# A two-layer attention and FFN kernel: the opening attention by halves of the heads, context sums cleared at the start, and another order of the gated sums at the end

## The chip, the cores and the metric

The kernel runs on one core of a Trainium2 chip. The metric is the device time of one execution in microseconds (us). Engines are named as in the profile: PE multiplies matrices, DVE and ACT work on vectors, POOL (GpSimd) and SP issue DMAs beside other work.

## The reference

All arrays are f32. `x` and `ctx` are (16, 256, 256): 16 batches of 256 rows of width 256. The mask has one entry per batch, query and key. Two layers each add an attention and a feed-forward part to x, on a layer norm of x without weights.

```python
# layer 0: 16 heads of width 16, keys = values = ctx
q, k, v = heads(layernorm(x)), heads(ctx), heads(ctx)
scores = where(mask == 0, -1e20, einsum('bqhd,bkhd->bhqk', q, k))
attn = softmax(scores / sqrt(256), axis=3)
x = x + einsum('bhqk,bkhd->bqhd', attn, v).reshape(b, l, e) @ W_out.T + b_out
# layer 0 FFN, 256 -> 1024 -> 256; quantization scales need the maximum over all activations
x = x + quant_linear(relu(quant_linear(layernorm(x), w1, b1)), w2, b2)
# layer 1: correlation of q and k by FFT, its mean over batches picks 6 delays, softmax over them,
# then the values shifted by these delays, weighted and projected
x = x + autocorrelation(layernorm(x), ctx, Wq, Wk, Wv, Wo, ...)
# layer 1 FFN: a shared expert, and 8 routed ones of which each token takes 2
t = layernorm(x)
shared = gelu(t @ Wfc_s + bfc_s) @ Wproj_s + bproj_s
routed = sum over e of gate[:, e] * (gelu(t @ Wfc[e] + bfc[e]) @ Wproj[e] + bproj[e])
x = x + shared + routed
```

## The kernel before, in words

x stays in SBUF for the whole program, as 32 tiles of 128 rows. PE's order inside the first attention is written out by hand, piece by piece; the other engines' orders come from a scheduler, which is held by "issue after" edges in places (`behind()` places an instruction after the last reduction issued). SP's queue issues its DMAs in order: an issue that has to wait holds up all behind it.

**Layer 0 attention.** Each batch has 16 heads in four groups of four. `prep(b)` spreads ctx on 32-partition strips (`cxp`, POOL, L431), normalizes x to `qp` (L440), turns the int mask into an added bf16 mask `mb` (DVE, L451), and turns `cxp` and `qp` on PE into `kT` and `qT`. `turn` (L369) does half of such a turn: four transposes into a PSUM tile of a pool with one buffer, and an ACT copy out (L374). `mtp` (L479) turns the mask.

`largest(b, r)` is a *round*: 16 score matmuls (`sp`, L498) into two tiles of the PSUM pool `ps_w` (three buffers) and eight DVE instructions that add the mask and take the row maximum (L509, into `mx`). Four rounds make a batch: `qt, gp = divmod(r, 2)`, so rounds 0 and 1 take the first 128 queries for both halves of the groups, rounds 2 and 3 the other 128. `shift(b)` negates the maxima into `mxc` (L529), turns them on PE (`mxtp`, L538) and writes them into spare rows of `qT` (L547), so that the second score matmul gives scores less their maximum.

A *slot* is one group of a batch. `weights(b, g)` computes transposed scores (`st`, 16 matmuls, L566), adds the mask by four matmuls (L576) and takes two exponentials on ACT (L586). `values` multiplies by the context (`o`, L599) one slot later. `finish(b)`, in pieces spread over the slots of the next batch, transposes `oT` (`otp`, L617), divides by the sums (L624, L625), transposes again (`ontp`, L635), copies on ACT (L641), projects (`pp`, L649) and adds to x (L653). `stats0` computes layer norm statistics ahead. Rounds run ahead of the slots: five rounds ahead from slot 2 on, four in the beginning. Before slot 0 the program does the rounds 0 to 3 of batch 0, with `prep(1)` and the statistics of batch 1 between, and then `shift(0)`.

**Transition to the first FFN.** `keys1(b)` loads ctx, transposes it (`ctp`, L942), copies it reversed to `cT` on ACT (L945), which also sums it into a column of `csum`; then it computes projected keys (`pk`, L954) and stores them in `gT` (ACT, L962). `csum`, and two constants `zsel` and `avg` that the autocorrelation uses much later, are allocated in a pool that takes over the attention's space, and are cleared there on POOL (L875 to L884). Four `keys1` and four `values1` come ahead of the first quantized block (`qi` L995/996, `qtp` L1000, `ph` L927, `hmax` L1008), whose scale needs the maximum over all x (POOL `partition_all_reduce`, L869).

**Tail.** The last part runs the shared expert in 16 units of 256 rows; units 12 to 15 are left for the end, beside the combination of the routed experts' outputs. `shared_fc(u)` (`pfs`, L1512, then gelu L1520), then one unit later `shared_proj(u)` (`pps`, L1552, a PSUM tile for two halves of 128 rows in a pool with two buffers). For the late units each half is added to x by itself (L1561) and sent out (`leave`, L1542). `combine(u)` loads the unit's routed outputs (`yg`, 512 KB, L1686), adds a bias row (L1693) and adds four gated products (L1698). Late units and combines are interleaved by these lines:

```python
pend, late_ones = None, list(range(U0, NU)) + list(range(U0))   # U0 = 12, NU = 16
share = -(-NU // (NU - U0))
```

After each `shared_fc` of a late unit, and after the previous unit's projection, four combines of this list follow; units 0 to 11 are sent out after theirs.

Of the kernel before, what the change touches and what calls it, by code (L numbers as in the profile page):

```python
# [8 lines left out]
F32 = mybir.dt.float32  # L9
# [19 lines left out]
def tile_kernel(ctx: ExitStack, tc: tile.TileContext, io: dict, out: bass.AP):  # L29
# [112 lines left out]

    rows_of = [32 * (b % 4) + b // 4 for b in range(B)]


# [3 lines left out]
    with tc.tile_pool(name="pa", bufs=2) as pa, tc.tile_pool(  # L149
# [213 lines left out]
        mxcs = [pa.tile([P, QT, 4, HP], F32, tag=f"mxc{i}", bufs=1, name=f"mxc{i}") for i in range(2)]  # L363
        def turn(dst, src, g0, name):

            tp = mtile([P, 2, QT, P], f"{name}_tp")
            for g in range(2):
                for t in range(QT):
                    nc.tensor.transpose(  # L369
                        tp[:, g, t, :],  # L370
                        src[:, t, 4 * (g0 + g) : 4 * (g0 + g) + 4, :].rearrange("p h d -> p (h d)"),
                        ident,
                    )
            nc.scalar.copy(  # L374
                dst[:, g0 : g0 + 2, :].rearrange("p g s -> p (g s)"),
                tp.rearrange("p g t q -> p (g t q)"),
            )
# [39 lines left out]
        def prep(b):  # L417
# [30 lines left out]
            if b == 0:  # L448
                order["last"] = last.ins
            with behind():  # L450
                nc.vector.tensor_scalar(mb, mi, 0.0, MASKED, ALU.is_equal, ALU.mult)  # L451
            if b == 2:
# [5 lines left out]
            if near:  # L458
                turn_close(kT, cx, f"kT{b}")
                yield  # L460
                turn_close(qT, qn, f"qT{b}")
                if b + 2 < B:
                    fetch(b + 2)
                yield
            else:
                turn(kT, cxp, 0, f"kT{b}")
                yield
                turn(kT, cxp, 2, f"kT{b}")
                yield
            if b == 0:  # L470
                turn(qT, qp, 0, f"qT{b}")
                yield
                turn(qT, qp, 2, f"qT{b}")
                yield
# [8 lines left out]
            yield  # L483
            if 0 < b < 3:
                turn(qT, qp, 0, f"qT{b}")
                yield
                turn(qT, qp, 2, f"qT{b}")
                yield

        def largest(b, r):  # L490

            pr = seqs[b]
            qt, gp = divmod(r, 2)
            sps = [ps_w.tile([P, 2, 2, S], F32, tag="w", name=f"sp{b}_{r}_{j}") for j in range(2)]
# [26 lines left out]

        def shift(b):

            pr = seqs[b]
            mxc = mxcs[b % 2]
            if b < 2:
                nc.gpsimd.memset(mxc, 0.0)
            with tc.high_priority():
                nc.vector.tensor_scalar(  # L529
                    mxc[:, :, :, HD : HD + G],  # L530
                    pr["mx"].rearrange("p t (g j) -> p t j g", g=G),
                    -1.0,
                    None,
                    ALU.mult,
                )
            tp = mtile([P, QT, P], f"mxtp{b}")
            for t in range(QT):
                nc.tensor.transpose(  # L538
                    tp[:, t, :], mxc[:, t].rearrange("p j c -> p (j c)"), ident
                )  # L540
            with ExitStack() as where:
                where.enter_context(tc.high_priority())
                if b > 0:
                    where.enter_context(tc.issue_after(order["half"]))
                for gs in (slice(0, 1), slice(1, G)) if b == 0 else (slice(0, G),):
                    to = pr["qT"][:, gs, :]
                    done = nc.vector.scalar_tensor_tensor(  # L547
                        to,
                        to,
                        keep,  # L550
                        tp.rearrange("p t q -> p (t q)").unsqueeze(1).to_broadcast(to.shape),
                        ALU.mult,
                        ALU.add,
                    ).ins
            if b == 0:
                order["last"] = done
            yield
# [116 lines left out]
        stats0(0, 1)  # L674
        first_prep = prep(0)
        piece(first_prep)
        load_x(1, 2)
        for _ in range(3):
            piece(first_prep)
        largest(0, 0)  # L680
        piece(first_prep)
        with behind():
            stats0(1, 2)
        first_prep = prep(1)
        piece(first_prep)
        largest(0, 1)
        piece(first_prep)
        piece(first_prep)
        fetch(2)
        load_x(2, 5)  # L690
        fetch(3)
        largest(0, 2)
        largest(0, 3)

# [29 lines left out]
        def load_w(name, eng):  # L724
# [16 lines left out]

        iota_l = early.tile([P, S], F32, name="iota_l")
        nc.gpsimd.iota(
            iota_l, pattern=[[1, S]], base=0, channel_multiplier=0, allow_small_or_imprecise_dtypes=True
        )

# [56 lines left out]

        for _ in shift(0):
            pass
        with behind():
            stats0(2, 3)
        load_x(5, 9)
        pend = None
        for b in range(B + 1):  # L810
            nxt = prep(b + 2) if b + 2 < B else rest
            fin = finish(b - 1) if b > 0 else None
            shf = shift(b + 1) if b + 1 < B else None
            past = summary(b - 2) if b > 1 else None

            jobs = [
                ((nxt,), (rest,), (fin,)),
                ((nxt,), (nxt,), (fin,)),
                ((fin,), (rest,), (fin,)),
                ((shf,), (), (fin,)),  # L820
            ]
            if b == 0:
                jobs = [
                    ((), (), (first_prep,)),
                    ((nxt,), (nxt,), (nxt,)),
                    ((nxt,), (nxt,), (rest,)),
                    ((rest,), (shf,), (rest,)),
                ]
            for r in range(4):

                n = 4 * b + r
                front, later = {0: ([], [4]), 1: ([5], [6])}.get(
                    n, ([n + 5] if n + 5 < 4 * B else [], [])
                )
                for m in front:
                    largest(*divmod(m, 4))
                for job in jobs[r][0]:
                    piece(job)
                if pend is not None:
                    values(*pend)  # L840
                for job in jobs[r][1]:
                    piece(job)
                pend = (b, r, []) if b < B else None
                wts = weights(*pend) if b < B else None
                piece(wts)
                for job in jobs[r][2]:
                    piece(job)
                piece(wts)
                if n == 0:
                    piece(first_prep)  # L850
                for m in later:
                    largest(*divmod(m, 4))
                with behind():
# [3 lines left out]
                    if b > 0 and r != 2:  # L857
                        piece(ints)
                if r == 0 and b % 4 == 0 and b + 9 < B:
                    load_x(b + 9, b + 13)  # L860
# [12 lines left out]
    gp = until_moe.enter_context(tc.tile_pool(name="gp", bufs=1, side="right"))  # L873
    csum = gp.tile([P, DC, P], F32, name="csum")
    nc.gpsimd.memset(csum, 0.0)  # L875

    zsel = gp.tile([P, 63], F32, name="zsel")
    nc.gpsimd.memset(zsel, 0.0)
    nc.gpsimd.memset(zsel[:, 31:32], 1.0 / D)

    avg = gp.tile([P, P], F32, name="avg")
    nc.gpsimd.memset(avg, 0.0)
    for j in range(4):
        nc.gpsimd.memset(avg[32 * j : 32 * j + B // 4, :], 1.0 / B)  # L884

# [242 lines left out]
    with tc.tile_pool(name="pc", bufs=2) as pc:  # L1128

        def diagonals(four):  # L1130

            for b, skew in four:
# [8 lines left out]
                )  # L1141

        queue = []
        for _ in range(3):
# [401 lines left out]
    def shared_proj(u, hT):  # L1546
        wp = shared_w[1]
        t0 = 2 * u
        po = ps_p.tile([P, 2, D], F32, tag="p", name=f"pps{u}")
        for i in range(2):  # L1550
            for fc in range(FC):
                nc.tensor.matmul(  # L1552
# [5 lines left out]
                )  # L1558
            if u >= U0:
                xt = x[:, t0 + i, :]  # L1560
                nc.vector.tensor_tensor(xt, po[:, i, :], xt, ALU.add)  # L1561
                leave(t0 + i)
        if u < U0:
            xu = x[:, t0 : t0 + 2, :]
# [80 lines left out]
    for u in range(U0):  # L1645
# [9 lines left out]
        pend = (u, hT)  # L1655
    shared_proj(*pend)
    until_moe.close()
    mw = ctx.enter_context(tc.tile_pool(name="mw", bufs=3, side="right"))
# [20 lines left out]
    def combine(u):  # L1679
# [11 lines left out]
        )  # L1691
        xu = x[:, t0 : t0 + 2, :]
        nc.vector.tensor_tensor(  # L1693
            xu, xu, bps_row.unsqueeze(1).to_broadcast([P, 2, D]), ALU.add
        )
        for t in range(2):
# [10 lines left out]

    pend, late_ones = None, list(range(U0, NU)) + list(range(U0))
    share = -(-NU // (NU - U0))
    for u in range(U0, NU):  # L1710
        hT = shared_fc(u)
        if pend is not None:
            shared_proj(*pend)
        pend = (u, hT)
        for v in late_ones[:share]:
            combine(v)
            if v < U0:
                leave(2 * v)
                leave(2 * v + 1)
        late_ones = late_ones[share:]  # L1720
    shared_proj(*pend)
# [39 lines left out]
```

## Time and profile before

| | |
|---|---|
| three runs | 1445.36, 1446.9, 1444.29 us, median 1445.36 |
| profiled execution | 1446.0 us, of which the span of the profile is 1444.3 us, at a mean granted clock of 0.987 |
| busy, share of the span | PE 1371.0 us (95%), DVE 642.9 (45%), ACT 539.6 (37%), POOL 239.1 (17%) |
| first st (slot 0) starts | 32.52 us |
| first keys (pk) start | 429.48 us |
| last x add starts | 1440.76 us |

A span counts from the first to the last instruction of the profiled execution, all positions are microseconds from its start, and shares of the span are averages over stages that have different limits. In a timeline a row gives the start, the length, the engine, the line, the operation with its tiles and how many were merged (x), and in brackets the idle time before it and what released it. Rows of waits give the total, the number of times and the longest.

### The profile page before, as it was taken

What the parts mean: (1) busy time and instruction counts of PE and PEld (TensorE: products, weight loads), DVE (VectorE), ACT (ScalarE), POOL (GpSimd) and SP (SyncE); (2) the same over time, 40 slices, a digit from 0 to 9 for tenths busy, and PEclk for the clock granted to TensorE, in tenths of its full rate; (3) what the DMA queues carried; (4) which work ended last, traced back from release to release, by engine and by line L of the source; (5) the groups of instructions that cost most, each with busy time, mean ns of one, the idle gap of its engine ahead of it and who ended that gap; (6) DMA issues with size and microseconds to landing.
All of it is one profiled execution on the core that took longest, in us unless ns stands there. A gap on an engine that the chain in (4) does not pass through costs nothing. (4 is left out here: it accounts for less than half of the span.)

```text
span 1444.3 us, 24031 instructions
## 1 busy us (share of the span) xinstructions
PE 1371.0 (95%) x8881; PEld 1041.8 (72%) x8955; DVE 642.9 (45%) x2553; ACT 539.6 (37%) x1019; POOL 239.1 (17%) x312
## 2 busy tenths in 40 slices
PE   6999999999988899999999999999999999999968
PEld 3566655666546544678688888888888888888857
DVE  7688879887736858847831101011011011011052
ACT  1454545454434367523623222332333333332221
POOL 6233033302000000000025540111111111111100
PEclk9899999999989999999999999999999999999989
DMA  9232323221001100233002245776767767764173
GB/s 276 69 93 65 91 82 102 62 75 21 12 8 45 37 8 1 88 118 86 10 27 74 77 138 201 249 235 240 254 226 245 258 229 242 254 227 167 54 239 116
DMA packets 127832, 184.07 MB, mean 127 GB/s; under 512 B 11600, under 2 KB 104952, under 8 KB 127712
## 3 DMA queue, kind: packets, MB, share of 16 engines
q1 hardware_dynamic: 117600, 152.55, 32.6%
q0 software_dynamic: 10112, 29.94, 6.1%
q8 instruction: 72, 1.18, 0.3%
q14 instruction: 48, 0.39, 0.1%
HBM read 141.16 MB, written 34.48 MB: 122 GB/s over the span
## 5 line engine op out<-in xcount | busy, mean ns | idle before, releaser
L1520 ACT ACTIVATE hTr<-pfr,bsel 128x256 f32<-128x256 f32 (+1 forms) x344 | 147.8, 430 | 345.7 <-PE pfr L1512 336.8
L1611 PE MATMUL ppr<-wp,hTr 128*128 128x256 f32 x1088 | 248.5, 379 | 0.0
L1512 PE MATMUL pfr<-xjT,wf 128*128 128x256 f32 (+1 forms) x1376 | 246.6, 338 | 0.7 <-DVE xjT L1601 0.7
L1512 PEld LDWEIGHTS pfr<-xjT,wf 128*128 128x128 f32 x1376 | 215.8, 191 | 30.3 <-issue 9.9
L1619 DVE TENSOR_TENSOR yj<-ppr,bj 128x512 f32<-128x512 f32 (+1 forms) x43 | 24.9, 580 | 440.3 <-PE ppr L1611 440.3
L1611 PEld LDWEIGHTS ppr<-wp,hTr 128*128 128x128 f32 x1088 | 202.2, 190 | 25.0
L509 DVE CUSTOM_DVE_ANT_0 junk<-sp,mb 128x256 bf16<-128x256 f32 x512 | 182.8, 420 | 37.7 <-PE sp L498 37.4
L586 ACT ACTIVATE pT<-st 128x1024 f32<-128x1024 f32 x128 | 124.4, 1021 | 128.0 <-PE st L576 128.0
L1637 POOL DMA_INDIRECT ys_d<-yj,to x68 | 65.4, 962 | 454.2 <-DVE to L1628 238.2
L1552 PE MATMUL pps<-wp-1_7259,hTs 128*128 128x256 f32 x512 | 117.4, 388 | 13.5 <-DVE x L1561 13.5
L1552 PEld LDWEIGHTS pps<-wp-1_7259,hTs 128*128 128x128 f32 x512 | 99.3, 195 | 28.7 <-DVE x L1561 14.7
L1520 ACT ACTIVATE hTs<-pfs,bcol 128x256 f32<-128x256 f32 x128 | 59.9, 474 | 160.1 <-PE pfs L1512 157.0
L1512 PE MATMUL pfs<-xnT,wf-1_7257 128*128 128x256 f32 x512 | 114.7, 380 | 0.1
L1512 PEld LDWEIGHTS pfs<-xnT,wf-1_7257 128*128 128x128 f32 x512 | 96.6, 190 | 14.2 <-issue 1.4
L498 PE MATMUL sp<-kT,qT 16*128 16x256 f32 x1024 | 93.1, 421 | 3.6 <-DVE mx L509 3.3
L566 PE MATMUL st<-qT,kT 32*128 32x256 f32 x1024 | 79.5, 408 | 0.7 <-DVE qT L547 0.7
L498 PEld LDWEIGHTS sp<-kT,qT 16*128 16x128 f32 x1024 | 59.2, 193 | 26.4 <-DVE mx L509 9.5
L1475 POOL DMA_INDIRECT xs_d<-xn,slot_i x64 | 61.8, 966 | 92.7 <-ACT hTs L1520 49.6
L927 PE MATMUL ph<-qT,w1T 128*128 128x512 bf16 x245 | 68.6, 378 | 7.4 <-DVE hmax L1008 2.8
L599 PE MATMUL o<-pT,cxp 128*32 128x256 f32 x1024 | 73.4, 396 | 1.3 <-ACT pT L586 1.3
L1565 DVE TENSOR_TENSOR x<-pps,x 128x512 f32<-128x512 f32 x12 | 8.3, 690 | 128.0 <-PE pps L1552 128.0
L566 PEld LDWEIGHTS st<-qT,kT 32*128 32x128 f32 x1024 | 51.4, 189 | 18.5 <-issue 12.6
(304 smaller groups left out, 1622.0 us busy)
## 6 DMA issues: line engine op xcount, KB each, us to landing
wf<-in_L_ffn_Wfc_dram SPq DMA_DIRECT2D x43, 1024.0 KB
wp<-in_L_ffn_Wproj_dram SPq DMA_DIRECT2D x43, 1024.0 KB, 5.5
xs_d<-zero POOLq DMA_DIRECT2D x36, 258.0 KB
yg<-ys_d SPq DMA_DIRECT2D x16, 512.0 KB, 6.2
xj<-xs_d SPq DMA_DIRECT2D x25, 258.0 KB
bj<-in_L_ffn_bproj_dram SPq DMA_DIRECT2D x43, 128.0 KB, 6.6
x<-in_x_dram SPq DMA_DIRECT2D x16, 256.0 KB, 9.0
cx<-in_ctx_dram SPq DMA_DIRECT2D x16, 256.0 KB, 2.8
```

Source lines behind the costliest of these rows:

```text
L498: nc.tensor.matmul(sps[j // 2][:, j % 2, g, :], pr["qT"][rows, 2 * gp + g, qt * P : (qt + 1) * P], pr["kT"][rows, 2 * gp + g, :], start=Tr ...
L509: order["last"] = done = nc.vector.tensor_tensor_reduce(out=junk, in0=sps[j // 2][:, j % 2, g, :], in1=pr["mb"][:, qt, :], scale=1.0, scal ...
L566: nc.tensor.matmul(tps[j // 2][:, j % 2, k, :], pr["kT"][rows, g, k * P : (k + 1) * P], pr["qT"][rows, g, :], start=(k == 0), stop=False, ...
L586: nc.scalar.activation(pT, tps[i], AF.Exp)
L599: nc.tensor.matmul(pr["o"][HP * j : HP * (j + 1), g % 2, :], pr["cxp"][:, k, 4 * g + j, :], pTs[j // 2][:, j % 2, k, :], start=(k == 0), s ...
L927: nc.tensor.matmul(ph, w1T[:, c, fc * P : (fc + 1) * P], qT[:, c, blk * 512 : (blk + 1) * 512], start=(c == 0), stop=(c == DC - 1),)
L1475: ins = nc.gpsimd.indirect_dma_start(out=xs_d, out_offset=bass.IndirectOffsetOnAxis(ap=slot_i[:, k, t : t + 1], axis=0), in_=xn3[t // QT][ ...
L1512: nc.tensor.matmul(ph, wf[:, c, fc * P : (fc + 1) * P], rhs[:, c, :], start=(c == 0), stop=(c == DC - 1),)
L1520: nc.scalar.activation(hT[:, fc, :n], ph, AF.Gelu_apprx_tanh, bias=bias[:, fc : fc + 1]).ins
L1552: nc.tensor.matmul(po[:, i, :], hT[:, fc, i * P : (i + 1) * P], wp[:, fc, :], start=(fc == 0), stop=(fc == FC - 1),)
L1611: nc.tensor.matmul(po[:, i, :], hT[:, fc, i * P : (i + 1) * P], wp[:, fc, :], start=(fc == 0), stop=(fc == FC - 1),)
L1637: nc.gpsimd.indirect_dma_start(out=ys_d, out_offset=bass.IndirectOffsetOnAxis(ap=to[:, i : i + 1], axis=0), in_=yj[:, i, :], in_offset=None,)
```

## The change

There are three parts.

1. *Opening.* In batch 0 both halves of a turn are written into one `ps_w` tile. `divmod` is swapped, so rounds 0 and 1 take all queries of the first eight heads. `shift` works on a half of the groups for batch 0: one half ahead of round 3, the other inside slot 0. The order of slots is a list with explicit round numbers; four rounds are ahead in the first slots, five from slot 8 on. The statistics of batch 1 stand before round 0 and its mask after round 3. `mxc` is cleared at the start.
2. *Transition.* `csum` is in a pool of the start and is cleared there. `zsel`, `avg` and `iota_l` are set up later, where the autocorrelation begins.
3. *Tail.* Units up to 14 are added to x as wholes and sent out after their combine; unit 15's second half has a PSUM tile of its own. The combines go 0, 1, 2; 3, 4, 12, 5; 6, 7, 13, 8; 9, 15, 10, 14, 11 after the four `shared_fc`. The bias row is added in a loop ahead of the routed experts' space. Seen from the instruction orders, DVE has these additions at the same places as before, while SP's queue has the first three `yg` loads, and then each further one behind out writes of earlier units.

```diff
+    csum = early.tile([P, DC, P], F32, name="csum")
+    nc.gpsimd.memset(csum, 0.0)
...
+        for t_ in mxcs:
+            nc.gpsimd.memset(t_, 0.0)
+        def turn(dst, src, g0, name, tp=None):
+            if tp is None:
+                tp = mtile([P, 2, QT, P], f"{name}_tp")
+            else:
+                tp = tp[:, g0 // 2].rearrange("p g (t q) -> p g t q", q=P)
...
+                tps = [
+                    ps_w.tile([P, 2, 2, S], F32, tag="w", name=f"{n}T0_tp") if b == 0 else None
+                    for n in "kq"
+                ]
+                turn(kT, cxp, 0, f"kT{b}", tps[0])
...
         def largest(b, r):
-            qt, gp = divmod(r, 2)
+            gp, qt = divmod(r, 2)
...
-        def shift(b):
+        def shift(b, gs=slice(0, G)):
             pr = seqs[b]
             mxc = mxcs[b % 2]
-            if b < 2:
-                nc.gpsimd.memset(mxc, 0.0)
...
         stats0(0, 1)
-        first_prep = prep(0)
-        piece(first_prep)
+        p0 = prep(0)
+        piece(p0)
         load_x(1, 2)
-        for _ in range(3):
-            piece(first_prep)
-        largest(0, 0)
-        piece(first_prep)
+        piece(p0)
         with behind():
             stats0(1, 2)
-        first_prep = prep(1)
-        piece(first_prep)
+        p1 = prep(1)
+        piece(p1)
+        piece(p0)
+        piece(p0)
+        largest(0, 0)
+        piece(p1)
         largest(0, 1)
-        piece(first_prep)
-        piece(first_prep)
+        piece(p0)
+        piece(p1)
         fetch(2)
         load_x(2, 5)
         fetch(3)
         largest(0, 2)
-        largest(0, 3)
...
-        for _ in shift(0):
+        for _ in shift(0, slice(0, G // 2)):
             pass
+        largest(0, 3)
+        piece(p1)
         with behind():
             stats0(2, 3)
...
+            if b == 0:
+                slots = [
+                    ["weights", p1, "more", 4, "shift"],
+                    ["sums", "weights", "p2", "more", 5, "p2"],
+                    ["sums", rest, "weights", "p2", "more", 6, "p2"],
+                    ["sums", rest, "weights", "p2", "more", 7, rest, 8, shf],
+                ]
+            elif b == 1:
+                slots = [
+                    [nxt, "sums", rest, "weights", fin, "more", 9],
+                    [nxt, "sums", nxt, "weights", fin, "more", 10],
+                    [fin, "sums", rest, "weights", fin, "more", 11],
+                    ["sums", "weights", fin, "more", 12, shf],
+                ]
...
-    csum = gp.tile([P, DC, P], F32, name="csum")
-    nc.gpsimd.memset(csum, 0.0)
-    zsel = gp.tile([P, 63], F32, name="zsel")
...
-    avg = gp.tile([P, P], F32, name="avg")
...
         po = ps_p.tile([P, 2, D], F32, tag="p", name=f"pps{u}")
         for i in range(2):
+            if u == NU - 1 and i == 1:
+                po = ps_p.tile([P, 2, D], F32, tag="p", name=f"pps{u}b")
...
-            if u >= U0:
+            if u == NU - 1:
                 xt = x[:, t0 + i, :]
                 nc.vector.tensor_tensor(xt, po[:, i, :], xt, ALU.add)
                 leave(t0 + i)
-        if u < U0:
+        if u < NU - 1:
             xu = x[:, t0 : t0 + 2, :]
             nc.vector.tensor_tensor(xu, po, xu, ALU.add)
...
+    for u in range(NU):
+        xu = x[:, 2 * u : 2 * u + 2, :]
+        nc.vector.tensor_tensor(xu, xu, bps_row.unsqueeze(1).to_broadcast([P, 2, D]), ALU.add)
     until_moe.close()
...
-    pend, late_ones = None, list(range(U0, NU)) + list(range(U0))
-    share = -(-NU // (NU - U0))
+    late_ones = list(range(U0))
+    share = -(-U0 // (NU - U0))
+    pend = None
     for u in range(U0, NU):
         hT = shared_fc(u)
         if pend is not None:
             shared_proj(*pend)
+            late_ones.insert(2, pend[0])
         pend = (u, hT)
-        for v in late_ones[:share]:
+        n = share + (u > U0)
+        if u == NU - 1:
+            late_ones.insert(1, u)
+            n = len(late_ones)
+        for v in late_ones[:n]:
             combine(v)
-            if v < U0:
+            if v < NU - 1:
                 leave(2 * v)
                 leave(2 * v + 1)
-        late_ones = late_ones[share:]
+        late_ones = late_ones[n:]
     shared_proj(*pend)
```

## The prediction

> **What bounds the kernel now.** I read the page first. Its rows of busy tenths say where a change can pay at all.
>
> ```profile
> ## 2 busy tenths in 40 slices
> PE   6999999999988899999999999999999999999968
> PEclk9899999999989999999999999999999999999989
> DMA  9232323221001100233002245776767767764173
> ```
>
> A slice is 36.1 us. PE is at 9 nearly everywhere (1371.0 us of the span of 1444.3), so only work that keeps PE waiting or cold counts. The low slices are the first (6), slices 11 to 13 (8, around 400 to 450 us) and the last but one (6). The change touches just these three places. I take them in order, reading the timeline, the windows and then the waits.
>
> Opening, timeline of DVE and PE:
>
> ```profile
> 21.79 0.42 DVE L509 CUSTOM_DVE_ANT_0 junk<-sp,mb 128x256 bf16<-128x256 f32 x1
> 32.52 2.09 PE L566 MATMUL st<-qT,kT 32*128 32x256 f32 x16 [0.66 <-DVE qT L547]
> 39.85 0.42 DVE L509 CUSTOM_DVE_ANT_0 junk<-sp,mb 128x256 bf16<-128x256 f32 x1 [3.41 <-PE sp L498]
> ```
>
> Round 0 reduces on DVE from 13.87 to 16.7, but round 1 starts only at 21.79: statistics and the mask of batch 1 stand between. The first weights (st) wait for all four rounds and the shift, until 32.52. Then DVE idles 3.41 us, and PE falls cold: granted clock 0.66 from 40 to 50 us.
>
> Transition to the first FFN, timeline of POOL, ACT and PE:
>
> ```profile
> 419.02 0.60 PE L942 MATMUL ctp<-ident,ck 128*128 128x128 f32 x4
> 428.61 0.31 POOL L875 MEMSET csum<- 128x256 f32 x1 [94.20 <-PE pp L649]
> 428.95 0.39 ACT L945 ACTIVATE cT<-ctp 128x256 f32<-128x256 f32 x1 [5.33 <-POOL csum L875]
> 429.48 3.78 PE L954 MATMUL pk<-cT,wkq 128*128 128x256 f32 x8 [1.07 <-ACT cT L945]
> ```
>
> The first context transposes end at 419.62. ACT's copy adds into csum, whose memset waits for the attention's space, freed by the last pp. So the keys start at 429.48, on a cold clock.
>
> Tail, waits of PE and timelines:
>
> ```profile
> PE pps L1552 <- DVE x L1561: 13.5, 3, 11.3
> 1380.59 3.25 DVE L1698 SCALAR_TENSOR_TENSOR x<-yg,gw,x 128x256 f32<-128x256 f32 x8 [10.67 <-DMA yg<-ys_d]
> 1399.28 1.22 PE L1552 MATMUL pps<-wp-1_7259,hTs 128*128 128x256 f32 x2 [11.27 <-DVE x L1561]
> 1440.76 0.42 DVE L1561 TENSOR_TENSOR x<-pps,x 128x256 f32<-128x256 f32 x1 [3.81 <-PE pps L1552]
> ```
>
> The second half of pps12 waits 11.27 us for DVE's add of the first half, which stands in DVE's order behind combines, and these wait for yg from memory. PE then runs cold (0.62 granted from 1390 to 1400).
>
> **The change, part by part.** The profiled execution took 1446.0 us (1.7 outside the span), 0.64 above the median of the runs, 1445.36. Sums go against 1446.0 and are then lowered by 0.6.
>
> *Opening.* Removed ahead of st_0: statistics and mask from between rounds 0 and 1 (16.7 to 21.79, 5.1 us). The statistics (about 3.3 us: 2 of 0.42, 2 of 0.17, 11 of 0.19) move into DVE's wait for sp_0 (4.18 idle before 13.87). The shift needs only rounds 0 and 1 for the first heads, and st_0 uses only those. The turns of kT and qT lose two waits of 0.7 for ACT; a batch-1 turn of 1.1 takes their place on PE. So I have round 0 at about 13.3, round 1 ending at 19.3, the negated maxima, round 2 and the half shift by 23.8 (8 x 0.345 = 2.77 a round, shift 0.23 + 1.1), and st_0, behind sp_3 on PE, ending near 26 (25.0 to 26.9) where it ended at 34.6: 8.6 earlier. Added: one more negate, pair of transposes (0.66) and shift in slot 0, which lie under the rounds. The three early memsets on POOL, some 1.0 us, lie in its 1.90 idle before 4.39; uncovered they would cost 1.0. POOL's loads and clears behind the earlier qp wait some 6 us more; their users come after 30 us, so nothing.
>
> From st_0 to st_8, where both orders are the same again, both kernels have nine rounds to reduce. Before that took 57.6 us (34.6 to 92.18). A slot is 5.85 when warm (st starts at 63.02, 68.90, 74.74), so eight are 46.8; on DVE the bound is its work from 30.7 to 92.18, 44.9, at the busy share that it reaches (26.01 of 29.16, 0.89): 50.5. The cold part (41 to 47.5 and 54.3 to 57.5 at half speed) is worth some 4.8. The stretch may keep its 57.6 (only 8.6 gained, less 1.5 if st_1 waits for its half shift: 7), or come down to 50.5 (gain 16). I take 11, nearer the lower end, because four cold slots are no shorter merely by starting earlier. The 92.18 to 138.5 stretch has PE busy 45.05 of 46.32, so the gain is handed on.
>
> *Transition.* csum is cleared at the start, so cT0 can follow ctp0 at about 420 instead of 428.95. The order on PE becomes ctp0, otp, pk0 in halves, otp, ctp1, ontp, pp, pk1, and so on. Work that was serial (9.5 us of the finish with PE idle between links, then keys at 3.29 a batch) overlaps. pk0 and most of pk1 fit into the gaps: 7.5 us is my sum for when qtp starts, 442.9 for 450.57. Ends: the 9.3 that cT0 moves less nothing hidden, and 4, if the clock falls all the same and pk and pp run at 3.78 and 2.07 for 2 and 1.03 (1.8 + 2 x 1.04 lost, 3.9, from 7.5 to 9). pk1 behind gT0 on ACT may hold pp_1 back 0.5 to 1.5; who waits for that is x's add, g and the all_reduce, then qi(0), ready at 440.04 where DVE idled from 445.05 to 452.09. 7 us of cover, so nothing. The other memsets and iota_l move to before the same reduction on POOL: still 1.5 us.
>
> The windows show the clock falling to 0.50 from 424 us, after 420 to 424 with PE busy 0.63 and 0.95 of 2.00 each; 436 to 438, busy 1.14, kept 1.00. With pk0 in that stretch I expect about 1.00. The Trainium skill ("TensorE: Matmul & The Clock Gate", Part 4) says that transposes do not count as busy for the gate in the way matmuls do; much of what fills these gaps is transposes, so by the rule the clock would still fall and this part would be worth about 4 and not 7.5. No row here separates the two.
>
> *Tail.* Combined adds per unit and no half-unit dependence: pps12 needs no DVE any more, pps14 only add12, the first half of pps15 only add13, its second half add14 (two PSUM buffers). PE's work from 1369.21 is 4 x (6.945 + 7.0) = 55.8, so it could end at 1425.0 against 1440.73: 15.7. The adds of bps_row stay where DVE already had them: nothing. Combines are 1.67 each, as now.
>
> What can be late is yg. SP issues in order, and each read from the fourth now stands behind out writes that wait for combines; only three reads go ahead where seven did. Walking the chain with 4 us from issue to DVE's use (the chain's rows 3.85, 3.93, 4.32) gives add12 at 1399.8 (needed 1411), add13 at 1412.7 (needed 1418), add14 at 1419.6 (needed 1422.5): no loss. With 6.20, the chain's longest but one, add13 comes at 1424 and add14 at 1430, PE ends near 1434, and 6 is left. I take 14, nearer the rows of 4, because fewer reads fly together. The rule that speaks against this: the skill's "DMA: Bandwidth & Descriptors", Rules for kernel authors, wants DMAs issued early and awaited late, and the change issues them later. By its fit for another queue (2.0 us and bytes over 436 GB/s, an estimate of 3.2 for 512 KB) the reads would still be in time and the full 15.7 would come.
>
> Sum: 11 + 7.5 + 14 = 32.5 off 1446.0: 1413.5, less 0.6: 1413.
>
> **The rivals.**
> 1. *Late reads in the tail*: landings of 6.2, the other parts as above: gain 24.5, 1421. For: the tile view's median to landing is 6.2. Against: that was with seven in flight.
> 2. *The early gains are half absorbed*: opening 7, transition 4, tail 14: 1420. For: DVE at 0.89 in the steady stretch, and a clock that falls. Both rivals together: 17, 1428.
> 3. *The other side, slower*: reads and writes on SP become one serial chain that is the bound of the tail. A trip is issue 0.44, two writes 0.82, landing 4 and a combine of 1.67: 6.9. Thirteen in series from 1380 make 90 us, an end of 1470, against 1444.3 less 18.5: net 7 slower, about 1452. It decides once almost every read is behind the writes of the unit just combined; with six landings in series each would have to take 12. SP's order has five reads going out in pairs, so I give this little.
> 4. *Less than it says*: gains under 3, if all three gaps are only moved to the next wait. Each gap has different causes, so it needs three failures.
>
> **How the numbers follow.** Forecast 0.52 (1403 to 1418: its parts at 16, 9 and 15.7 give 40.7 at best, 1404.6), rival 1 0.18, rival 2 0.16, both 0.07, rival 4 0.02, rival 3 0.05. Range 1403 to 1428, which leaves out the last two and some of the edge. 0.2% is 2.9 us, about what a measurement of this kernel can tell from no change. Faster: 0.93; same 0.02; slower 0.05.
>
> **What would show it.** Right: st_0 ending by 27 and st_8 by 83; cT0 near 420, no PE clock of 0.50 between 424 and 430, and qtp some 18 us earlier than 450.57 in all; in the tail no wait of pps above 3, and the last x add 3 to 4 us before the end. Wrong: DVE idle over 5 us between rounds 0 and 4; pp cold; yg waits on DVE of more than 5 each, followed by PE waiting at pps14 or pps15. A time above 1428 would say that a second wait stood behind one of the three.

## The result, and the profile after

The changed kernel took 1422.57 us (median of four runs, 1422.12 to 1424.23) against 1444.82 for the kernel before on the same chip: a ratio of 0.9847, 95% interval 0.983 to 0.9864, or 22.3 us less where 32.4 were forecast. Its profiled execution took 1422.67, with a span of 1421.0, so the two spans differ by 23.3.

The page after, its rows of busy tenths (slices of 35.5 us):

```profile
PE   7899998999988899999999999999999999999998
PEclk9999999999999999999999999999999999999999
DMA  8422223220001100233002225777677677775347
```

The last but one PE slice is now full, and the clock row has no 8 left. Slices 12 to 14 are low as before, the first has gone from 6 to 7, and two have lost a tenth: slice 2 (35.5 to 71 us, slots 3 and 4) and slice 7 (213 to 249, slot 31). Where the 23.3 us come from is read best from one event after another, at the same place of both programs:

| event | before, us | after, us | lead |
|---|---|---|---|
| st of slot 0 | 32.52 | 27.02 | 5.5 |
| st of slot 3 | 63.02 | 46.83 | 16.2 |
| st of slot 4 | 68.90 | 59.79 | 9.1 |
| st of slot 8 | 92.18 | 87.40 | 4.8 |
| st of slot 31 | 235.54 | 230.73 | 4.8 |
| st of slot 32 | 241.59 | 240.62 | 1.0 |
| st of slot 63, the last | 413.99 | 413.07 | 0.9 |
| first qtp | 450.78 | 441.16 | 9.6 |
| first pfs of unit 12 | 1369.21 | 1360.28 | 8.9 |
| end of the span | 1444.3 | 1421.0 | 23.3 |

At slot 3 the lead flatters: the kernel before has nine rounds of scores behind it there, the changed one seven, and a round is 1.5 us of PE. At slot 8 both have done the same. So the opening gave 4.8 and then lost 3.9 of it, the transition gave 8.7, 0.7 went between the first qtp and unit 12, and the tail gave 14.4 (75.1 to 60.7 from the first pfs of unit 12 to the end).

Opening, timeline of the changed kernel (DVE and PE):

```profile
7.05 1.12 PE L376 MATMUL kT_tp<-ident,cxp 128*128 128x128 f32 x4 [0.68 <-ACT kT L381]
17.47 0.42 DVE L531 CUSTOM_DVE_ANT_0 junk<-sp,mb 128x256 bf16<-128x256 f32 x1 [0.23 <-PE sp L520]
20.42 2.53 DVE L549 TENSOR_SCALAR mxc<-mx 128x16 f32<-128x16 f32 x1
27.02 2.49 PE L580 MATMUL st<-qT,kT 32*128 32x256 f32 x16
56.26 1.12 PE L392 MATMUL kT_tp<-ident,cx 128*128 128x128 f32 x4 [1.81 <-DVE qT L563]
```

Round 1 follows round 0 (17.47 where it was 21.79). The negation that I priced at 0.23 took 2.53. The second half of the turn of kT still waits 0.68 for ACT's copy of the first, and so does that of qT at 11.23: the two waits that I had taken off are there. The first st took 2.49, half speed (1.15 at slot 3), and ended at 29.5 where I had 26. At slot 4 PE waits 1.81 for the shift of batch 1.

Transition, timeline, and the windows view (length, PE busy, weight loads, DVE, ACT, POOL, granted clock, DMA share, GB/s):

```profile
418.11 0.60 PE L951 MATMUL ctp<-ident,ck 128*128 128x128 f32 x4
418.79 0.38 ACT L954 ACTIVATE cT<-ctp 128x256 f32<-128x256 f32 x1 [0.26 <-PE ctp L951]
419.32 1.13 PE L963 MATMUL pk<-cT,wkq 128*128 128x256 f32 x4 [0.29 <-ACT cT L954]
418.00:430.00 12.00, 10.60 (x56) 8.23 (x56) 5.97 (x23) 5.11 (x18) 1.24 (x6) 1.00 0.26 68
```

cT follows the turn at once, pk comes 10.2 us earlier, and the clock stays at 1.00 in the twelve microseconds where it had been 0.71 on average.

Tail: rows of PE's and DVE's waits, of the yg tile's view, and of the timeline:

```profile
PE pps15b L1576 <- DVE x L1590: 1.3, 1, 1.3
DVE x L1723 <- DMA yg<-ys_d: 25.9, 10, 10.6
DMA to landing us min/median/max: 4.9/5.9/6.9
1413.67 3.72 PE L1576 MATMUL pps15b<-wp-1_7250,hTs 128*128 128x256 f32 x16 [1.35 <-DVE x L1590]
1417.43 0.42 DVE L1586 TENSOR_TENSOR x<-pps15b,x 128x256 f32<-128x256 f32 x1 [1.77 <-PE pps15b L1576]
```

PE's 13.5 us of waits have become 1.35, its clock no longer falls, and the end is again 3.6 us behind PE.

### The profile page after: what moved, and what is told of

Its sections match the earlier page's. It is cut to its first block, busy times and chain, and to the rows that moved or that the text cites. A ratio compares the mean times of both kernels' runs of the same rounds, so it can differ in the third digit from the quotient of the medians.

```text
span 1421.0 us, 24034 instructions
## 1 busy us (share of the span) xinstructions
PE 1365.8 (96%) x8883; PEld 1039.5 (73%) x8957; DVE 646.3 (45%) x2551; ACT 539.1 (38%) x1019; POOL 237.6 (17%) x312
## 4 chain that ended last, share of the span: by engine, by line
PE 80%; DVE 10%; DMA 4%; issue 2%; ACT 2%; SPq 1%; POOL 0%; DVEq 0%; another core or an unknown queue 0%; ACTq 0%; POOLq 0%
PE pfr L1534 17%; PE ppr L1636 16%; PE pps L1576 5%; PE pfs L1534 5%; PE sp L520 5%; PE st L580 5%; PE o L613 4%; PE st L590 3%; PE ph L936 3%; PE pm L1189 2%; DMA ys_d<-yj,to 2%; DMA yg<-ys_d 2%; PE pk L963 2%; PE po L1304 2%; PE pp L663 2%
## 5 line engine op out<-in xcount | busy, mean ns | idle before, releaser
L1576 PE MATMUL pps<-wp-1_7250,hTs 128*128 128x256 f32 x496 | 109.8, 379 | 0.0
L1576 PEld LDWEIGHTS pps<-wp-1_7250,hTs 128*128 128x128 f32 x496 | 94.1, 190 | 12.7
L520 PEld LDWEIGHTS sp<-kT,qT 16*128 16x128 f32 x1024 | 59.1, 194 | 21.3 <-issue 9.0
```

Source lines behind the costliest of these rows:

```text
L520: nc.tensor.matmul(sps[j // 2][:, j % 2, g, :], pr["qT"][rows, 2 * gp + g, qt * P : (qt + 1) * P], pr["kT"][rows, 2 * gp + g, :], start=Tr ...
L1576: nc.tensor.matmul(po[:, i, :], hT[:, fc, i * P : (i + 1) * P], wp[:, fc, :], start=(fc == 0), stop=(fc == FC - 1),)
```

## The experiments

In all of them the times stand beside runs of the kernel before on the same chip, and the traces are compared at the events of the table. A kernel's own runs spread by 2 to 9 us, mostly 2 to 5, so differences of 2 us between medians are read from the trace or not at all.

**One part undone at a time.** The lists of edits are those of the change, with one of the three parts left as it was before.

> The changed kernel with the opening of the kernel before (transition and tail as changed). The prediction's term: the opening is worth 11, so 1422.6 + 11 = 1433.6 us. What the starts of st say in the two traces: the lead is 16.2 us at slot 3, 4.8 from slot 8 to slot 31 and 0.9 from slot 32 on, because at slot 31 of the changed kernel one DVE instruction took 3.36 us instead of 0.83 beside POOL. By that the time is about 1423.5, with no such long instruction in this run's trace (w_w at L207 under 1 us); if it is there again, 1427.4.

> The changed kernel with csum, zsel, avg and iota_l where they were before. The prediction's term is 7.5: 1430.1 us. By the traces (last st 0.9 earlier, qtp 9.6 earlier) the part is worth 8.7: 1431.3, with cT behind the csum memset again and the granted clock at 0.50 from about 423 us. Rival: qtp does not set the time because of the cover on DVE; then under 4: below 1426.6.

> The changed kernel with the tail of the kernel before. The prediction's term is 14: 1436.6 us; by the traces (23.3 in all, 9.0 ahead when the tail begins) 14.3: 1436.9, with one wait of pps of about 11 us. Rival of the late reads: 6, so 1428.6.

Measured: with the old opening 1420.17 us (0.9817 of the kernel before, 0.9801 to 0.9834), with the old transition 1429.05 (0.9899, 0.9866 to 0.9932), with the old tail 1435.7 (0.9925, 0.9905 to 0.9945). Against 1422.57 the transition is worth 6.5 and the tail 13.1; the opening fails to bring its 11, since without it the kernel is no slower (2.4 less, which is within the spread). The expectation for it (1423.5) was 3.3 too high, and its trace says why: at the last st it is 4.1 us ahead of the kernel before, although up to there only the early clear of csum and the place of iota_l on POOL differ. It is 1.2 ahead at slot 0 and 1.0 at slot 8; the other 3.1 come by slot 31. One place is at 137 us, where two DVE instructions of the integer weights that took 2.67 together in the trace of before took 1.10; another is a cold window near 195 us that did not come. So the same attention runs 3 to 4 us shorter or longer by meetings of engines and by the phase of the clock's windows, and an opening worth less than that can't be read from times alone.

With the old transition, csum's memset is at 428.66 again and the clock at 0.50 for 10.2 us from 423.2; from the last st to the first qtp it takes 36.8 us, as before, for 28.1 in the changed kernel. In that run the lead of slot 0 was 8.9 (st at 23.65), and slot 2 was still no earlier (lead 16.0 as in the changed kernel). The opening is the same in both; what differs is PE's speed. Round 0 on PE, in the changed kernel's timeline and then in that of old_transition:

```profile
12.28 2.09 PE L520 MATMUL sp<-kT,qT 16*128 16x256 f32 x16
```

```profile
11.47 1.15 PE L518 MATMUL sp<-kT,qT 16*128 16x256 f32 x16
```

The clock row reads 1.00 for both here, but the durations show half speed in the changed kernel, up to its round 4 at 31.7 us. Why PE was faster in the one than in the other stays open.

**The loss at slot 31.** In the changed kernel's timeline:

```profile
233.64 3.36 DVE L207 TENSOR_SCALAR w_w<-w_w 128x1024 f32<-128x1024 f32 x1
233.68 2.77 POOL L659 TENSOR_TENSOR x<-x,row_L_xattn_b_out 128x256 f32<-128x256 f32 x4
237.39 1.11 PE L392 MATMUL kT_tp<-ident,cx 128*128 128x128 f32 x4 [2.34 <-DVE x L667]
```

The same two in the timeline of the kernel before:

```profile
238.25 0.83 DVE L205 TENSOR_SCALAR w_w<-w_w 128x1024 f32<-128x1024 f32 x1
238.51 3.22 POOL L645 TENSOR_TENSOR x<-x,row_L_xattn_b_out 128x256 f32<-128x256 f32 x4
```

Where DVE starts 0.26 us ahead of POOL's four additions it takes 0.83; 0.04 ahead, it takes 3.36 and ends 0.55 after the last of them. It is no single case: in the attention of the fourteen traces, 34 DVE instructions other than the masked maxima took over 1 us more than usual for their kind and shape, and 33 of them ended 0.03 to 0.55 us after the end of a run of POOL instructions that follow one behind another. The addition of pp to x waits behind it, PE's next turn waits for that (2.34; the transposes have a single PSUM buffer), and then runs cold.

```diff
-                    if b > 0 and r != 2:
+                    if b > 0 and r != 2 and n != 31:
                         piece(ints)
```

> The changed kernel, with the piece of the integer weights of slot 31 (L207 on DVE, 128x1024 f32) left to the next slot; all is computed. Theory of the shared access of DVE and POOL: the 2.5 us that this instruction waited for POOL's four x additions, and the cold 3.4 us window after it, go; st of slot 32 starts about 3.8 us earlier (lead of 4.8 kept), 1418.8 us, if no other long DVE instruction meets POOL. Rival, the clock gate's window alone (its phase came to lie badly, and DVE was incidental): the cold window at 237 us stays, and the time is within 1 us of 1422.6.

Measured 1418.53 us (0.9814, 0.9797 to 0.983), expected 1418.8. The lead at slot 32 is 5.0, there is no cold window at 237, and the turn of slot 32 stands without a wait:

```profile
234.75 0.65 PE L392 MATMUL kT_tp<-ident,cx 128*128 128x128 f32 x4
```

So the wait for POOL was the cause of this loss, and the clock's fall its consequence.

**The loss between slots 3 and 8.** Each of the two places with two rounds in a row (7 and 8 at slot 3; 12 and 13, one behind the other between slots 7 and 8) is followed by half clock. The first experiment puts the sums (o) between rounds 12 and 13; the second also moves round 7 ahead of st; the third leaves the order alone and adds work.

```diff
# w8
-                    [5, nxt, "sums", rest, "weights", fin, "more"],
+                    [nxt, "sums", 5, rest, "weights", fin, "more"] if b == 2 else [5, nxt, ...],
# w38, besides
-                    ["sums", rest, "weights", "p2", "more", 7, rest, 8, shf],
+                    ["sums", 7, "p2", rest, "weights", "more", 8, shf],
# dummies, in largest(), warm=4 for rounds 8 and 13
+            for _ in range(warm):
+                nc.tensor.matmul(sps[0][:, 0, 0, :], ident, pr["kT"][:, 0, :], start=True, stop=True)
```

> As skip31, but at slot 8 round 13 comes after the sums of slot 7 (o) instead of straight behind round 12; all is computed. Theory of the gate by kind of work: a 3.4 us window that holds only score rounds and transposes is followed by half clock, however busy PE is; round 13 behind round 12 made such a window (80.4 to 83.8 in the changed kernel). With o between, no fall of the clock near 83 us, and st of slot 8 starts about 2.5 us earlier relative to st of slot 7 (10.8 falls to about 8.3); time 1416. Rival, PE waits there for DVE's reductions: the step from slot 7 to 8 stays above 10 and the time at 1418.5.

> As w8, and in slot 3 round 7 stands ahead of st instead of straight ahead of round 8; all is computed. Gate theory: no clock of 0.50 between 50 and 60 us, step from slot 3 to slot 4 near 9 instead of 13.0, slot 8 some 5 us ahead of w8's, time 1411. Rival: st of slot 3 now waits for round 7's reductions (two of three buffers), so what the clock gives is lost there, and the time is that of w8.

> As skip31, with four added 128x256 f32 matmuls of all 128 rows ahead of round 8 and four ahead of round 13 (they write what the round overwrites; nothing else changes), about 1.0 us of PE work each time. Gate theory by kind of work: the two cold windows near 53 and 83 us vanish although PE has more to do and waits as long, st of slot 8 starts no later than in skip31 (87.6) and up to 3 us earlier, time 1415.5 to 1418.5. Rival, the gate goes by idle time or busy time alone: both cold stretches stay, slot 8 is 2 to 4 us later, time 1420.5 to 1422.5.

Measured: w8 1423.48 (0.985, 0.983 to 0.9869), w38 1418.65 (0.981, 0.9789 to 0.9831), dummies 1420.38 (0.9829, 0.981 to 0.9848). The first two missed. PE's timeline in w8, then in w38:

```profile
83.92 1.12 PE L392 MATMUL kT_tp<-ident,cx 128*128 128x128 f32 x4 [2.40 <-DVE qT L563]
```

```profile
49.04 1.62 PE L580 MATMUL st<-qT,kT 32*128 32x256 f32 x16
55.87 1.12 PE L392 MATMUL kT_tp<-ident,cx 128*128 128x128 f32 x4 [2.00 <-DVE qT L563]
```

The next batch's turn needs the one PSUM buffer in which the turned maxima (mxtp) wait for DVE's shift. Round 13 had been filling this wait; with it gone PE stood idle for 2.40 us and was cold for 17.1. In w38 the step from slot 3 to 4 did fall, from 12.7 in w8 to 9.8, but st of slot 3 came 2.3 later, and slot 8 is where it was in w8 (89.39 for 89.47): the rival was right there. Its time was not that of w8, though, but 4.8 less: from slot 8 to unit 12 its trace gains 4.0 us, and two cold windows of w8 (199 and 725 us) are missing there.

The third separates kinds of work from busy time. The windows view of the changed kernel, along the clock's own windows of 3.41 us:

```profile
49.65:53.07 3.42, 2.98 (x33) 1.76 (x29) 2.58 (x15) 1.56 (x3) 0.00 (x0) 1.00 0.00 0
53.07:56.48 3.41, 0.95 (x5) 0.51 (x4) 3.41 (x16) 0.00 (x0) 0.00 (x0) 0.50 0.02 5
80.37:83.79 3.42, 2.84 (x34) 1.65 (x30) 3.02 (x12) 0.53 (x1) 3.10 (x3) 1.00 0.03 7
83.79:87.20 3.41, 3.38 (x24) 1.59 (x22) 3.41 (x17) 0.73 (x2) 3.41 (x5) 0.50 0.27 63
```

PE is busy 2.98 and 2.84 of 3.42, nearly all of it score rounds and transposes, and the next window is at half clock. With the added matmuls, in the kernel called dummies:

```profile
50.87:54.29 3.42, 2.96 (x26) 1.91 (x24) 2.71 (x17) 0.00 (x0) 0.00 (x0) 1.00 0.00 0
81.60:85.01 3.41, 3.41 (x34) 2.34 (x36) 3.41 (x14) 0.14 (x1) 3.41 (x4) 1.00 0.00 0
85.01:88.42 3.41, 3.06 (x35) 1.56 (x28) 3.41 (x18) 1.30 (x3) 3.41 (x6) 1.00 0.40 106
```

The four added matmuls took 1.99 us at the one place and 1.89 at the other, not the 1.0 that I expected, so they add 3.9 us. The window from 50.87 is no busier than that from 49.65 in the changed kernel (2.96 and 2.98), holds 1.51 us of the added work and is followed by full clock. The fall near 83 us is gone too, that near 53 is one window at 57.7 (after a window in which PE was idle for 1.9 us), and slot 8 comes at 86.13 for 87.59 with 3.9 us more work. The time did not follow, since this kernel's tail happened to take 63.9 us (below).

From 37 us to the last st, the fourteen traces have 1462 such windows that began at full clock. In 33 of them the clock fell at the end. All but one of these had at most 0.60 us of matmuls other than score rounds and transposes; the other had 0.90, with PE idle for more than half of it. The only windows with 0.60 or less that kept the clock are four that hold 1.5 to 2.1 us of the added matmuls. Busy time does not sort them: a window busy for 2.58 us with 0.70 of other matmuls kept its clock (apart, 183.9), those busy for 2.98 with 0.10 or less lost it.

**The tail's reads.** Here out writes are held back by three combines, so that reads of yg stand ahead of them.

```diff
             combine(v)
             if v < NU - 1:
+                held.append(v)
+            while len(held) > (3 if u < NU - 1 or v != late_ones[n - 1] else 0):
+                w = held.pop(0)
-                leave(2 * v)
-                leave(2 * v + 1)
+                leave(2 * w)
+                leave(2 * w + 1)
```

> As skip31, with the out writes of a unit issued three combines later, so that reads of yg stand ahead of them (six reads before most waits instead of three); all is computed. Theory that SP's order holds the reads back: the wait of pps15b for DVE (1.3 us) goes, PE's work from the first pfs of unit 12 (55.8) is the bound, the tail from there to the span's end falls from 60.4 to about 59, time 1417. Rival, the reads are bound by the memory's rate: DVE waits as long for yg and the tail is 60.4 or more, the late writes adding up to 2 us at the end.

Measured 1417.45 us (0.9809, 0.9788 to 0.983). The tail took 59.08 us, and 59.1 in all five kernels with this order, against 60.1 to 63.9 in the seven with the changed kernel's. DVE's wait row, the tile's row and PE's last projection:

```profile
DVE x L1723 <- DMA yg<-ys_d: 20.4, 7, 10.5
DMA to landing us min/median/max: 4.7/5.1/5.9
1408.65 3.62 PE L1576 MATMUL pps15b<-wp-1_7250,hTs 128*128 128x256 f32 x16
```

No wait is left ahead of pps15b. In the kernels without this order it waited 0.7 to 3.1, and where it waited longest the clock fell too. Slow landings alone don't bring the wait: ahead9_warm, which has this order, has a median of 6.0 us to landing and no wait. So SP's order does hold the reads back, at a price of 1 to 5 us, well under the 8 that my rival gave it.

**The negation on ACT, and fewer places with two rounds.** All three of these have tail_reads as their base.

```diff
# mxc_act, for batch 0
+                    nc.scalar.activation(mxc[...], pr["mx"]..., AF.Copy, scale=-1.0)
# ahead9, batch 1 (ahead9_warm adds four matmuls ahead of rounds 8 and 9)
-                    [nxt, "sums", rest, "weights", fin, "more", 9],
+                    [9, nxt, "sums", rest, "weights", fin, "more"],
...
-                    ["sums", "weights", fin, "more", 12, shf],
+                    [12, shf, "sums", "weights", fin, "more"],
```

> As tail_reads, with batch 0's two negations of the maxima on ACT instead of DVE; all is computed. In the changed kernel the first of them took 2.53 us on DVE (20.42 to 22.95) while POOL cleared and filled cxp; on ACT it should take some 0.3. The prediction's chain: st of slot 0 starts about 2 us earlier (24.7 for 26.8) and all later slots keep it: 1415.4 us. What old_transition suggests (st of slot 0 at 23.65, and slot 2 no earlier than in the changed kernel): slots 2 and 8 stay where they are, within 0.5, and the time is 1417.4.

> As tail_reads, with rounds 9 to 12 at the start of slots 4 to 7 instead of their ends; all is computed. Rounds and DVE work are the same, but the second catching up (rounds 12 and 13 in a row at slot 8) is gone, and round 9 stands where PE waited 1.8 us for the shift at slot 4. Theory of wait and cold window at each catching up: step from slot 7 to 8 about 6.2 instead of 10.8, slot 8 some 3 us earlier (84 for 87.1), time 1414.5. Rival, DVE is the bound there: rounds 7, 8 and 9 in a row take 8.3 us on it, st of slot 4 comes 3 us later, slot 8 is where it was, 1417.5.

> As ahead9, with four added 128x256 f32 matmuls of all rows ahead of rounds 8 and 9 (about 2.0 us of PE work, overwritten by the round). Gate theory by kind of work: the half clock that three rounds in a row bring between 50 and 62 us goes or is a window shorter, and slot 8 is no later than in ahead9 in spite of 2 us more work, 1413 to 1415. Rival, busy or idle time alone: same cold windows, 2 us later, 1416.5.

Measured: mxc_act 1415.65 us (0.9803, 0.9779 to 0.9826). The negation took 0.22 on ACT, and nothing came of it at slot 0:

```profile
20.45 2.09 PE L520 MATMUL sp<-kT,qT 16*128 16x256 f32 x16
21.04 0.22 ACT L550 ACTIVATE mxc<-mx 128x16 f32<-128x16 f32 x1
22.57 0.42 DVE L531 CUSTOM_DVE_ANT_0 junk<-sp,mb 128x256 bf16<-128x256 f32 x1 [2.14 <-PE sp L520]
27.15 2.44 PE L588 MATMUL st<-qT,kT 32*128 32x256 f32 x16
```

Round 2's matmuls run on PE from 20.45 at half speed, so DVE only waits 2.14 us for them instead. The time fell by 1.8 us, which is within the spread; in the trace slot 8 is 0.5 later than in tail_reads, and the last st is 2.3 earlier; on the way the long instruction at 133 us (2.41, here at most 0.82) and the cold window at 194 are absent.

ahead9: 1410.16 (0.976, 0.9738 to 0.9782), expected 1414.5. Slot 8's st:

```profile
84.47 1.15 PE L580 MATMUL st<-qT,kT 32*128 32x256 f32 x16
```

It comes 2.6 us earlier, the step from slot 7 to 8 is 6.2 where it was 10.8, and no cold window follows until 715 us. ahead9_warm took 1411.93 (0.977, 0.9747 to 0.9792): its windows stay warm where ahead9's fall for 6.8 us,

```profile
52.60:56.00 3.40, 3.40 (x28) 2.33 (x26) 2.69 (x15) 0.00 (x0) 0.00 (x0) 1.00 0.03 5
```

slot 8 is at 84.22, no later than in ahead9, and the added work uses up what the clock gives. In the trace it is 3.9 us, twice what I expected. The last run takes DVE and POOL apart everywhere:

```diff
-                    if b > 0 and r != 2 and n != 31:
+                    if b > 0 and r != 2 and n % 8 != 7:
                         piece(ints)
```

> As ahead9, with no piece of the integer weights on DVE in any slot 7, 15, 23 and so on, in which POOL adds the bias row to x right after normalizing the next queries; all is computed, each piece a slot later. Theory that DVE's plain tensor_scalar waits out POOL's run of instructions: the long ones of ahead9 (L202 2.41 us near 130, L213 1.62 near 180) are at their usual 0.35 and 0.62, PE's waits of 1.45 and 0.40 for the x addition behind them go, last st 1.9 us earlier (402.9), time 1408.3. Rival, they are long because of their data or place in their own sequence: they stay long a slot later, time 1410.2.

Measured 1410.94 us (0.9769, 0.975 to 0.9788). In the trace all went as expected: no instruction of the integer weights takes over 1.2 us, and the last st comes at 402.20 for 404.76 (402.9 expected). The times show no gain over ahead9; they can't tell 2 us here. The profiled executions were 1409.92 and 1412.97. Either of the two beats the changed kernel by about 12 us, the tail's reads and slot 31 included.

## Why the prediction was right, and where it was wrong

1422.57 lies in the range of 1403 to 1428, and the direction was right. But the forecast proper was 1403 to 1418, and the result lies outside it, where the rivals stood. The gain was 22.3 of 32.4, and one term of the sum is at fault. Of the signs named ahead, those of the opening failed (st_0 ended at 29.5 and not by 27, st_8 started at 87.4 and not by 83), and so qtp came 9.6 earlier and not 18; those of the transition's clock and of the tail held.

- *Tail, 14: 14.4 in the trace.* PE's work held: from the first pfs of unit 12 it is 55.5 us where it never waits (55.8 predicted). From issue to use the chain has 3.87, 4.59, 4.67, 6.93 and 5.91 us where I took 4 or 6.20 for all. So add14 started at 1412.93, 52.7 behind the first pfs of unit 12, between the 50.4 of the one walk and the 61 of the other; it takes 0.68 us, PE needed it done by 52.0, and the loss was 1.35. The rule of early DMAs did speak against the change, and is worth 1 to 5 us here.
- *Transition, 7.5: 8.7.* cT moved as said, and PE's clock did not fall: pk now stands between the transposes, as in the sum, and the fallback of 4 is refuted; no run shows that pk alone keeps the clock. (The first qtp of the kernel before starts at 450.78, not 450.57.) The cover on DVE held: DVE's waits for qtp fell from 11.6 to 4.5 us, and no new one appeared.
- *Opening, 11: 0.9 at the last st, and nothing in the times.* Three steps failed. First, "st_0, behind sp_3 on PE, ending near 26": it ended at 29.5. The two waits of 0.7 that the turns were to lose stayed, and round 0's first reduction came at 14.40 for 13.3. From there I had followed DVE, while PE ran its turns and rounds at half speed, round 2 behind a turn of batch 1 that waits 0.77 us for its single PSUM buffer; the 2.53 us negation lay beside that. With round 0 at full speed, in old_transition, st of slot 0 started 3.4 earlier. Second, "nearer the lower end" was still too good for the stretch to slot 8: it took 57.9 us (29.5 to 87.4), as long as before (57.6). The two places with two rounds each cost a wait for the shift and one or two cold windows. Third, "the gain is handed on" was argued from PE being busy 45.05 of 46.32 between 92 and 138. It was handed on to slot 31 and then lost to one DVE instruction that waited for POOL.

Of the rivals, the half absorbed gains came nearest with their total (1420), but by luck: they had 7 for the opening and 4 for the transition, where the trace has 0.9 and 8.7. The clock that falls, one of their reasons, did so in the opening and not in the transition. Late reads are real, but small. The serial chain on SP did not come.

What stays open is the opening's worth as such: between the kernels with the old one (1420.17) and with the changed one and slot 31 mended (1418.53) there is less than one kernel's spread, and at the last st their traces are 1.0 apart.

## What to carry to other kernels

A lead that is won early is only worth what is left at the next place where engines meet: compare the starts of the same instruction all through both traces before believing that it is handed on. Filling PE with matmuls of few rows (16 here) and transposes did not keep it fast: see to it that each few microseconds hold some work on many rows, and don't put all such rounds in a row. And where a queue issues reads and writes in order, put the reads a few steps ahead of writes that wait for compute.

## What the runs showed of the hardware

- The clock's windows are 3.41 us long (in the attention and the transition of the fourteen traces its cold stretches last 3.41, 6.83, 10.24 or 17.07 us), and what counts in them is not busy time. Score rounds (16 rows by 256 columns) with transposes brought half clock at 2.98 of 3.42 us busy; 1.51 us of 128-row matmuls in a window busy for 2.96 kept it whole. The Trainium skill ("TensorE: Matmul & The Clock Gate", Part 4) says of transposes that they don't count as matmuls do, and the runs agree (a window with 1.01 us of them and 1.91 of rounds lost its clock in old_transition, at 81.9); they show the same for matmuls of 16 rows.
- A plain tensor_scalar of DVE on f32 that met POOL's additions or clears waited for the whole run of them behind one another (3.36 us instead of 0.83 beside four additions of 2.77 in all), while the masked maxima on DVE kept their 0.42 beside POOL. The skill ("SBUF — State Buffer", Who interferes with whom) has the shared access of the two and that the second to come is blocked for the instruction; here it was blocked for four in a row, though by the profile DVE started first, by 0.04 us; where it started 0.26 ahead it was not blocked, so 0.2 us decided over 2.5.
